# Turning gathered expert tokens with VectorE and two DMAs instead of TensorE, in one fused attention and expert block

## The chip, the core and the metric

The kernel runs on one core of one Trainium2 chip. The metric is device microseconds (us) of one execution. A core has TensorE (PE in the profile; PEld are its weight loads), VectorE (DVE), ScalarE (ACT), GpSimd (POOL), SyncE (SP, which here only issues DMAs) and 16 DMA engines. Every engine runs its own instructions in the order in which the program gives them, and waits for others through semaphores.

## What is computed

One transformer block on x of shape (16, 256, 256) in float32: an attention part, then a part with eight experts, in which each expert takes the 512 tokens with its highest gate values out of 4096 tokens. Only the second part is touched:

```python
# x: (4096, 256) tokens after attention; E = 8 experts, DD = 1024
gate = softmax(tok @ Wgate.T, axis=-1)
vals, idx = top_k(gate.T, 512)                  # for each expert, its 512 tokens
g = ln(tok[idx], mlp_g, mlp_b)                  # gathered, normalised, gain and bias
y = gelu(g @ fc1[e].T + b1[e]) @ fc2[e].T + b2[e]
tok = tok.at[idx].add(y * vals)                 # scattered back, added
```

The attention part (16 sequences of 256 tokens, 16 heads of 64) is the same before and after the change.

## The kernel before

The kernel is one program whose instructions are put in order by hand (a list of places for the attention part, a loop for the experts); the framework adds semaphores and changes no order.

The attention part takes the sequences one after another and writes two things to DRAM for each token: the token itself, to `out`, and its normalised form without gain and bias, to `xn_dram` (4096 rows of 1 KB).

The expert part is a list of 16 jobs (`Job`). A job is one expert with 256 of its 512 tokens. Jobs 0 to 7 use a first routing, over the tokens of the first 15 sequences; jobs 8 to 15 use a second routing over all tokens, which is worked out beside jobs 1 to 6. The steps of a job are these:

- `load`: SyncE issues three DMAs, 1 MB for the second weight matrix, 1 MB for the first, 128 KB for the bias. The weight tiles have two buffers, so the load for job k+2 waits until job k's matmuls are done.
- `gives` and `onehot` (VectorE): one 128x128 one-hot matrix for each 128 tokens (30 of them for a job of the first routing, 32 for one of the second), from which `list_matmul` (TensorE) and `take` (VectorE) make the list of the job's token numbers and gate values.
- `gather` (GpSimd): two indirect DMAs fetch 2 x 128 rows of `xn_dram`.
- `transposes` (TensorE): four 128x128 transposes turn the gathered tokens, and `evict` (ScalarE) applies gain and bias from PSUM to SBUF (tile `xT`).
- `up` and `gelu` (8 steps f), `down` (two halves i of four steps each), `weigh` and `finish` (VectorE): the two layers and the scaling.
- `scatter` (GpSimd): for each half i an indirect DMA that adds 128 rows to `out`.

The expert loop runs over the jobs. Each round k has 16 slots s, eight for `up` and eight for `down` of job k. Between them stand the steps for the next job (`new` = job k+1) and the one after (`far` = job k+2). `LIST_AT` = 5 is the slot in which the list of `new` is made and its gathers are issued, `TURN_AT` = 14 the slot in which its tokens are turned. The one-hots of `far` are laid out one step (two or three matrices) for each slot, from slot 6 of one round to slot 4 of the next; what is left is laid out in front of `list_matmul`. Round 7 is different (`late`): job 8 needs the second routing, and all its one-hots are made in slots 0 to 5 of that round, its list in slot `LATE_AT` = 7. The generator `rest` does the second routing in rounds 1 to 6. In every fifth slot it has VectorE choose two bits of the threshold from TensorE's last count and compare for the next two (lines 1060 to 1090), and TensorE counts five slots later (line 1075).

The attention part has the same kind of turn as the change uses: VectorE transposes 32x32 blocks (line 861), one store takes the tile to DRAM (`blocks`, line 869), and one load with rearranged rows brings it back (line 882).

Of the kernel before, what the change touches and what calls it, by code (L numbers as in the profile page):

```python
# [9 lines left out]
F32 = mybir.dt.float32  # L10
I32 = mybir.dt.int32
BF16 = mybir.dt.bfloat16
AF = mybir.ActivationFunctionType
# [5 lines left out]
P = 128  # L19
B, N, D = 16, 256, 256  # L20
H, HD = 16, 64
E, DD = 8, 1024
# [5 lines left out]
DC = D // P  # L28
HP = H // 2
FC = DD // P  # L30
KC = CAP // P
KL = KC // 2
CAPL = CAP // 2
NV = 5
SQ = 32
QB = P // SQ
# [2 lines left out]

LN1_G, LN1_B, B_ADA, MLP_G, MLP_B = 0, 2, 4, 6, 8  # L40
QN_G, QN_B, KN_G, KN_B, B1 = 10, 11, 12, 13, 14
NVEC = B1 + E * FC


class Plan:
# [7 lines left out]
    def step(self, place, engine, took, run, needs=(), makes=(), tiles=(), mode=0, lag=0.1):  # L53
        k = len(self.steps)
        self.steps.append((place, engine, took, run, needs, tiles, mode, lag))
        for m in makes:
            self.makers.setdefault(m, []).append(k)
# [7 lines left out]
def kernel(  # L65
# [6 lines left out]
    woutT: bass.AP,  # L72
    wgateT: bass.AP,
    fc1T: bass.AP,
    fc2T: bass.AP,
    b2s: bass.AP,
    vecs: bass.AP,
# [2 lines left out]
    nc = tc.nc  # L80

    const = ctx.enter_context(tc.tile_pool(name="const", bufs=1))
    dram = ctx.enter_context(tc.tile_pool(name="dram", bufs=1, space=DRAM))
# [6 lines left out]
    vec = const.tile([P, NVEC], F32, name="vec")  # L90
# [440 lines left out]
    if True:  # L531
        attw = ctx.enter_context(tc.tile_pool(name="attw", bufs=1))
        seq = ctx.enter_context(tc.tile_pool(name="seq", bufs=2))
        work = ctx.enter_context(tc.tile_pool(name="work", bufs=2))
# [146 lines left out]
        class Group:  # L681
# [91 lines left out]

            def back(self):
                if self.g < 2:
                    self.raw = work.tile([P, QB, TB, HP // 2, SQ], F32, tag="qraw", bufs=2, name="qraw")
                else:
                    self.raw = self.keys()[:, self.g - 2]
                raw = self.raw.rearrange("p k t h m -> p k (t h m)")
                nc.sync.dma_start(raw, self.blocks.rearrange("k d q n -> (d q) k n"))  # L780

            def affine(self):
                if self.g < 2:
                    qT = of_sequence(qTs, self.b, "qT", [P, HP, N])
                    for t in range(TB):
                        nc.scalar.activation(
                            qT[:, 4 * self.g : 4 * self.g + 4, bass.ts(t, P)].rearrange(
                                "p h (k m) -> p k h m", m=SQ
                            ),
                            self.raw[:, :, t], AF.Identity, bias=qgb[:, 1:2], scale=qgb[:, 0:1],  # L790
                        )
                    return
                kT = self.raw.rearrange("p k t h m -> p (k t h m)")
                nc.scalar.activation(
                    kT, kT, AF.Identity,
                    bias=vec[:, KN_B : KN_B + 1], scale=vec[:, KN_G : KN_G + 1],
                )
# [399 lines left out]
        class Job:  # L1197
            def __init__(self, e, routing, tiles):
                self.e, self.routing, self.tiles = e, routing, tiles
                self.oh = None  # L1200

            def load(self):


                e = self.e
                self.w2 = seq.tile([P, FC, D], F32, tag="oT", name="w2")
                nc.sync.dma_start(self.w2, fc2T[e].rearrange("(f p) d -> p f d", p=P))
                self.w1 = seq.tile([P, DC, DD], F32, tag="v", bufs=2, name="w1")
                nc.sync.dma_start(self.w1, fc1T[e].rearrange("(c p) f -> p c f", p=P))
                self.b2 = moe.tile([P, D], F32, tag="b2", bufs=2, name="b2")  # L1210
                nc.sync.dma_start(self.b2, b2s[:, bass.ts(e, D)].to_broadcast([P, D]))

# [65 lines left out]
            def evict(self):  # L1278
                self.xT = seq.tile([P, DC, CAPL], F32, tag="hT", name="xT")
                for c in range(DC):  # L1280
                    nc.scalar.activation(
                        self.xT[:, c, :], self.px[:, c, :], AF.Identity,
                        bias=vec[:, MLP_B + c : MLP_B + c + 1],
                        scale=vec[:, MLP_G + c : MLP_G + c + 1],
                    )
                self.hid = seq.tile([P, FC, CAPL], F32, tag="qT", name="hid")
                self.y = work.tile([P, KL, D], F32, tag="pr", bufs=PRB, name="y")
                self.ph, self.py = {}, {}

            def up(self, f):  # L1290
                self.ph[f] = ps.tile([P, CAPL], F32, tag="sc", bufs=4, name="ph")
                for c in range(DC):
                    nc.tensor.matmul(  # L1293
                        self.ph[f], self.w1[:, c, bass.ts(f, P)], self.xT[:, c, :],
                        start=(c == 0), stop=(c == DC - 1),
                    )

            def gelu(self, f):
                k = B1 + self.e * FC + f
                nc.scalar.activation(  # L1300
                    self.hid[:, f, :], self.ph[f], AF.Gelu_apprx_tanh,
                    bias=vec[:, k : k + 1], scale=1.0,
                )

            def down(self, i, a=0, b=FC):
# [51 lines left out]
        for b in range(B):  # L1357
# [6 lines left out]
            a = First(b)  # L1364
# [9 lines left out]
            for (g, t), p in GROUP.items():  # L1374
                p += base
                a = Group(b, g, t)
                n = (b, g, t)
# [27 lines left out]
            for d in range(HP // 2):  # L1405
                a = Quad(b, d)
                p = base + d * QUAD
                g = d // 2
                n = (b, d)
                po = ("po", 0) + n  # L1410
                for i in range(2):
                    q = p + 3 * i
                    m = n + (i,)
                    sums, pb, prT, blocks = ("sums",) + m, ("pb",) + m, ("prT",) + m, ("blocks",) + m
# [20 lines left out]
            for t in range(TB):  # L1435
                a = Tail(b, t)
                p = base + TAIL[t]
                n = (b, t)
# [52 lines left out]
        jobs = [Job(e, r, n) for r, n in ((first, n1), (second, NT)) for e in range(E)]  # L1491
        for n in range(2):
            at(ROUTE + 60 + n * 80, "SP", 1.5, jobs[n].load, (), [("w", n)], [("oT", B + n), ("v", B + n)], lag=6.0)
        for n in range(2):
            a = jobs[n]
            k = top + 10 + 20 * n
# [29 lines left out]
        for k in plan.order(PLACES):  # L1526
            plan.steps[k][3]()

        LIST_AT, TURN_AT, LATE_AT = 5, 14, 7
        SLOTS = 2 * FC  # L1530

        def second_routing():
# [15 lines left out]

        rest = second_routing()
        last = len(jobs) // 2 - 2  # L1550
        jobs[2].load()
        parts = iter(())
        for k in range(1, len(jobs)):
            a = jobs[k]
            new = jobs[k + 1] if k + 1 < len(jobs) else None
            far = jobs[k + 2] if k + 2 < len(jobs) else None
            late = k == last + 1
            for s in range(SLOTS):
                for step in next(rest, ()):
                    step()  # L1560
                if late and s == 0:
                    new.gives()
                if late and s < 6:
                    new.onehot(6 * s, 6 * s + 6)
                if new and s == (LATE_AT if late else LIST_AT):
                    for _ in () if late else parts:
                        pass
                    new.list_matmul(0, NT)
                    new.take()
                    new.gather()  # L1570
                    if k == 1:
                        jobs[0].scatter(by_end[1])
                if new and s == TURN_AT:
                    new.transposes()
                    new.evict()
                if not late and s < LIST_AT:
                    next(parts, None)
                if far and k != last and s > LIST_AT:
                    if s == LIST_AT + 1:
                        parts = lay_out(far)  # L1580
                    next(parts)
                if s < FC:
                    a.up(s)
                    a.gelu(s)
                    if s == FC - 1:
                        a.weigh()
                else:
                    i, q = divmod(s - FC, 4)
                    a.down(i, 2 * q, 2 * q + 2)
                    if q == 3:  # L1590
                        a.finish(i)
                        a.scatter(i)
            if far:
                far.load()
        assert next(rest, None) is None
# [50 lines left out]
```

## Time and profile before

| what | value |
|---|---|
| time, median of 3 runs | 1074.48 us (1072.66 to 1075.8) |
| profiled execution: time, span | 1075.44 us, 1073.7 us |
| TensorE matmul busy, share of the span | 1039.4 us, 97% |
| VectorE busy | 822.4 us, 77% |
| ScalarE busy | 588.9 us, 55% |
| GpSimd busy | 617.5 us, 58% |
| DMA, all queues | 246.85 MB, mean 230 GB/s |

The span is the time from the first instruction to the last; the execution's own time is 1.7 us longer. The expert rounds 1 to 15 lie between 835 and 1067 us of the span. Queue q1 carries the DMAs that SyncE issues, q0 the indirect ones of GpSimd. In the timeline a row is a run of equal instructions with its start and duration in us, and in brackets the idle time of the engine before it and what ended that.

### The profile page before, as it was taken

The page shows a single profiled execution, that of the slowest core. Times are in us where ns is not written, and L with a number is a line of the kernel's source. Part 1 is how long each engine was busy: PE and PEld are TensorE (multiplying, and loading weights), DVE is VectorE, ACT ScalarE, POOL GpSimd, SP SyncE. Part 2 cuts the span into 40 slices and gives each one's busy share as a digit, 9 for nine tenths or more (in the row PEclk, how much of TensorE's full clock was granted, in tenths as well). Part 3 has the DMA queues.
Part 4 walks back from the last instruction along what each step waited for, and adds up shares of the span by engine and source line. Part 5 has one row for each costly group of instructions (what it writes and reads, how often), then busy time and mean ns, then how long its engine had stood idle before and what let it go on. Part 6 is the DMA issues. An engine that isn't in the chain of part 4 may idle for free. (4 is left out here: it accounts for less than half of the span.)

```text
span 1073.7 us, 17767 instructions
## 1 busy us (share of the span) xinstructions
PE 1039.4 (97%) x5547; PEld 681.8 (64%) x5547; DVE 822.4 (77%) x2281; ACT 588.9 (55%) x1646; POOL 617.5 (58%) x997
## 2 busy tenths in 40 slices
PE   7899999999999999999999999999789999999996
PEld 4455656555554655656565565666468888888885
DVE  6667888989888898798888888888667588655440
ACT  1577676666666666575766667675503422333331
POOL 3666776778667686766767676674401433333332
PEclk7999999999999999999999999999999999999998
DMA  6014889888987898888888898889430656665661
GB/s 217 1 60 157 279 289 319 293 294 277 309 281 262 282 317 303 294 291 271 280 296 304 280 306 282 290 315 312 147 103 21 196 146 180 196 184 155 185 204 20
DMA packets 165005, 246.85 MB, mean 230 GB/s; under 512 B 9520, under 2 KB 135728, under 8 KB 164912
## 3 DMA queue, kind: packets, MB, share of 16 engines
q1 hardware_dynamic: 156992, 235.44, 64.7%
q0 software_dynamic: 6144, 8.39, 4.3%
q10 hardware_dynamic: 1776, 1.90, 0.5%
q8 instruction: 44, 0.72, 0.3%
q14 instruction: 49, 0.40, 0.1%
HBM read 140.84 MB, written 104.86 MB: 229 GB/s over the span
## 5 line engine op out<-in xcount | busy, mean ns | idle before, releaser
L693 PE MATMUL pm<-wq,hT 128*128 128x512 f32 x768 | 362.0, 609 | 7.0 <-DVE qk L730 4.2
L851 POOL TENSOR_SCALAR pr<-pr,sums 128x256 f32<-128x256 f32 x512 | 238.2, 485 | 97.2 <-DVE sums L847 90.8
L840 ACT ACTIVATE pr<-sc,nmax 128x256 f32<-128x256 f32 x512 | 237.8, 480 | 101.5 <-DVE nmax L827 77.6
L693 PEld LDWEIGHTS pm<-wq,hT 128*128 128x128 f32 x768 | 138.2, 191 | 162.5 <-issue 137.2
L103 POOL TENSOR_TENSOR ss<-ss,neghalf 128x8 f32<-128x8 f32 x128 | 210.7, 1646 | 10.7
L827 DVE TENSOR_REDUCE nmax<-sc 128x2 f32<-128x512 f32 x256 | 165.8, 676 | 14.3 <-PE sc L819 13.6
L861 DVE STREAM_TRANSPOSE pb<-pr 128x512 f32<-128x512 f32 x232 | 154.2, 687 | 7.4 <-POOL pr L851 6.9
L819 PE MATMUL sc<-kT,qT 64*128 64x256 f32 x1024 | 135.2, 394 | 0.0
L907 PE MATMUL po<-prT,v 128*64 128x256 f32 x1024 | 128.7, 389 | 2.9 <-DMA prT<-blocks 2.9
L706 ACT ACTIVATE sq<-pm 128x512 f32<-128x512 f32 x128 | 76.7, 604 | 92.0 <-PE pm L693 91.0
L819 PEld LDWEIGHTS sc<-kT,qT 64*128 64x128 f32 x1024 | 91.3, 186 | 46.9 <-issue 28.5
L1326 POOL DMA_INDIRECT out<-y,idx x32 | 51.1, 1597 | 120.1 <-DVE y L1320 66.2
L1293 PE MATMUL ph<-xT,w 128*128 128x256 f32 x512 | 117.6, 383 | 0.0
L1309 PE MATMUL py<-w,hid 128*128 128x256 f32 x512 | 116.3, 380 | 0.0
L933 PE MATMUL pw<-wo,oT 128*128 128x256 f32 x512 | 115.2, 381 | 0.0
L907 PEld LDWEIGHTS po<-prT,v 128*64 128x64 f32 x1024 | 66.8, 137 | 68.7 <-issue 19.3
L933 PEld LDWEIGHTS pw<-wo,oT 128*128 128x128 f32 x512 | 96.3, 190 | 21.0 <-issue 5.8
L840 ACT ACTIVATION_READ_ACCUMULATOR pr<-sc,nmax 128x1 f32 x512 | 108.0, 211 | 0.0
L730 DVE TENSOR_TENSOR qk<-pm,ss 128x512 f32<-128x512 f32 x128 | 89.7, 702 | 22.8 <-POOL ss L103 20.8
L1300 ACT ACTIVATE hid<-ph,vec 128x256 f32<-128x256 f32 x128 | 60.4, 474 | 84.2 <-PE ph L1293 77.2
L1309 PEld LDWEIGHTS py<-w,hid 128*128 128x128 f32 x512 | 95.6, 190 | 12.8
L1293 PEld LDWEIGHTS ph<-xT,w 128*128 128x128 f32 x512 | 95.5, 190 | 12.9
(142 smaller groups left out, 1081.6 us busy)
## 6 DMA issues: line engine op xcount, KB each, us to landing
blocks<-pb SPq DMA_DIRECT2D x116, 512.0 KB
prT<-blocks SPq DMA_DIRECT2D x116, 512.0 KB
kblocks<-kb SPq DMA_DIRECT2D x60, 512.0 KB
w<-in_fc2T SPq DMA_DIRECT2D x16, 1024.0 KB
w<-in_fc1T SPq DMA_DIRECT2D x16, 1024.0 KB
qraw<-kblocks SPq DMA_DIRECT2D x30, 512.0 KB
kT<-kblocks SPq DMA_DIRECT2D x30, 512.0 KB
out<-tok SPq DMA_DIRECT2D x32, 128.0 KB
```

Of the source, the lines that this page charges most:

```text
L103: nc.gpsimd.tensor_tensor(dst, src, neghalf[:, : src.shape[1]], ALU.pow)
L693: nc.tensor.matmul(self.pm, hTs[self.b][:, c, bass.ts(self.t, P)], wq[:, c, bass.ts(self.g, GW)], start=(c == 0), stop=(c == DC - 1),)
L730: engine.tensor_tensor(dst, src.rearrange("p (q e d) -> p q e d", q=QB, e=8), by_head(self.ss[:, 1, :]), ALU.mult,)
L819: nc.tensor.matmul(self.sc[i, j][:, t, :], qTs[self.b][rows, hp, bass.ts(t, P)], keys[rows, hp] if whole else keys[rows, hp // 4, hp % 4], ...
L827: nc.vector.tensor_reduce(self.nmax[i, j], self.sc[i, j], AX.X, ALU.max, negate=True)
L840: nc.scalar.activation(dst, src, AF.Exp, bias=self.nmax[i, j][:, t : t + 1], scale=1.0, accum_out=self.sums[i][:, 0, j, t : t + 1],)
L851: nc.gpsimd.tensor_scalar(self.pr[i, j][:, t, :], self.pr[i, j][:, t, :], self.sums[i][:, 1, j, t : t + 1], 1.0, ALU.mult, ALU.mult,)
L861: nc.vector.transpose(self.pb[i][:, :, :, j].rearrange("p k c t n -> p t k c n"), self.pr[i, j].rearrange("p t (k c m) -> p t k c m", c=TB ...
L907: nc.tensor.matmul(self.po[j * HD : (j + 1) * HD, i, :], vs[self.b][:, c, bass.ts(4 * self.d + 2 * i + j, HD)], prT[:, j, c] if (self.b, s ...
L933: nc.tensor.matmul(self.pw, oTs[self.b][:, hp // 2, self.t, hp % 2, :], wo[:, hp, :], start=(hp == 0), stop=(hp == HP - 1),)
L1293: nc.tensor.matmul(self.ph[f], self.w1[:, c, bass.ts(f, P)], self.xT[:, c, :], start=(c == 0), stop=(c == DC - 1),)
L1309: nc.tensor.matmul(self.py[i], self.hid[:, f, bass.ts(i, P)], self.w2[:, f, :], start=(f == 0), stop=(f == FC - 1),)
```

## The change

For twelve of the 16 jobs (3 to 7 and 9 to 15, `job.exchanged`), the four TensorE transposes are replaced by an exchange. VectorE turns 32x32 blocks of the gathered tokens (`turn`, two instructions of 128x256), SyncE stores the tile to DRAM (`away`, 256 KB in rows of 2 KB), waits for it, and loads it back with the blocks at their places (`back`, 256 KB in runs of 512 B). ScalarE then applies gain and bias in place (`affine`). The order of the features that this gives is another one, and the first weight matrix, the gain and the bias are laid out to match on the host. The order of tokens within a job's columns is put right by `gelu`'s access pattern.

The order in the loop changes as well. The list is made and the gathers are issued in slot 0 (round 1 stays at 5, round 7 at 7), `turn`, `away` and `back` stand in slot 6, `affine` in slot 13. The second scatter of a job is held back and issued in slot 0 of the next round, behind the gathers. In round 1 two steps of one-hots are laid out for each slot.

```diff
+            def turn(self):
+                self.xb = work.tile([P, QB, DC, KL, SQ], F32, tag="prT", bufs=4, name="xb")
+                for i in range(KL):
+                    nc.vector.transpose(
+                        self.xb[:, :, :, i].rearrange("p q c n -> p c q n"),
+                        self.xg[:, i].rearrange("p (c q m) -> p c q m", c=DC, m=SQ),
+                    )
+
+            def away(self):
+                self.blocks = dram.tile([QB, SQ, QB, P], F32, tag="xblocks", bufs=2, name="xblocks")
+                nc.sync.dma_start(
+                    self.blocks.rearrange("k m q n -> (k m) (q n)"),
+                    self.xb.rearrange("p q c i n -> p (q c i n)"),
+                )
+
+            def back(self):
+                self.xT = seq.tile([P, QB, DC, KL, SQ], F32, tag="hT", name="xT")
+                nc.sync.dma_start(
+                    self.xT.rearrange("p k c i n -> p k (c i n)"),
+                    self.blocks.rearrange("k m q n -> (m q) k n"),
+                )
+
+            def affine(self):
+                for c in range(DC):
+                    xT = self.xT[:, :, c].rearrange("p k i n -> p k (i n)")
+                    nc.scalar.activation(
+                        xT, xT, AF.Identity,
+                        bias=vec[:, MLP_BQ + c : MLP_BQ + c + 1],
+                        scale=vec[:, MLP_GQ + c : MLP_GQ + c + 1],
+                    )
+                self.outputs()
...
-        LIST_AT, TURN_AT, LATE_AT = 5, 14, 7
+        LIST_AT, TURN_AT, LATE_AT = 0, 14, 7
+        EXCHANGE = {6: ("turn", "away", "back"), 13: ("affine",)}
...
+        for k, job in enumerate(jobs):
+            job.exchanged = k > 2 and k != last + 2
         jobs[2].load()
         parts = iter(())
+        held = []
         for k in range(1, len(jobs)):
...
             late = k == last + 1
+            list_at = LATE_AT if late else 5 if k == 1 else LIST_AT
             for s in range(SLOTS):
...
-                if new and s == (LATE_AT if late else LIST_AT):
+                if new and s == list_at:
                     for _ in () if late else parts:
                         pass
                     new.list_matmul(0, NT)
@@
+                if s == 0:
+                    for step in held:
+                        step()
+                    held = []
+                if new and new.exchanged:
+                    for what in EXCHANGE.get(s, ()):
+                        getattr(new, what)()
+                elif new and s == TURN_AT:
                     new.transposes()
                     new.evict()
-                if not late and s < LIST_AT:
+                if not late and s < list_at:
                     next(parts, None)
-                if far and k != last and s > LIST_AT:
-                    if s == LIST_AT + 1:
+                if far and k != last and s > list_at:
+                    if s == list_at + 1:
                         parts = lay_out(far)
-                    next(parts)
+                    for _ in range(2 if k == 1 else 1):
+                        next(parts, None)
@@
                         a.finish(i)
-                        a.scatter(i)
+                        if new and i == KL - 1:
+                            held = [partial(a.scatter, i)]
+                        else:
+                            a.scatter(i)
```

More of the change, by code (lines that the diff above doesn't have):

```diff
@@ L41 @@
 QN_G, QN_B, KN_G, KN_B, B1 = 10, 11, 12, 13, 14
-NVEC = B1 + E * FC
+MLP_GQ = B1 + E * FC
+MLP_BQ = MLP_GQ + 2
+NVEC = MLP_GQ + 4
 class Plan:
@@ L74 @@
     fc1T: bass.AP,
+    fc1Q: bass.AP,
     fc2T: bass.AP,
@@ L1200, in __init__ @@
                 self.oh = None
+                self.exchanged = False
             def load(self):
@@ L1208, in load @@
                 self.w1 = seq.tile([P, DC, DD], F32, tag="v", bufs=2, name="w1")
-                nc.sync.dma_start(self.w1, fc1T[e].rearrange("(c p) f -> p c f", p=P))
+                rows = fc1Q if self.exchanged else fc1T
+                nc.sync.dma_start(self.w1, rows[e].rearrange("(c p) f -> p c f", p=P))
                 self.b2 = moe.tile([P, D], F32, tag="b2", bufs=2, name="b2")
@@ L1285, in evict, with outputs @@
                     )
+                self.outputs()
[26 more added lines that the diff above has]
+                    )
+                self.outputs()
+            def outputs(self):
                 self.hid = seq.tile([P, FC, CAPL], F32, tag="qT", name="hid")
@@ L1293, in up @@
                     nc.tensor.matmul(
-                        self.ph[f], self.w1[:, c, bass.ts(f, P)], self.xT[:, c, :],
+                        self.ph[f], self.w1[:, c, bass.ts(f, P)],
+                        self.xT[:, :, c].rearrange("p k i n -> p k (i n)") if self.exchanged else self.xT[:, c, :],
                         start=(c == 0), stop=(c == DC - 1),
@@ L1299, in gelu @@
                 k = B1 + self.e * FC + f
+                dst, src = self.hid[:, f, :], self.ph[f]
+                if self.exchanged:
+                    dst = dst.rearrange("p (i k n) -> p k i n", i=KL, n=SQ)
+                    src = src.rearrange("p (k i n) -> p k i n", i=KL, n=SQ)
                 nc.scalar.activation(
-                    self.hid[:, f, :], self.ph[f], AF.Gelu_apprx_tanh,
-                    bias=vec[:, k : k + 1], scale=1.0,
+                    dst, src, AF.Gelu_apprx_tanh, bias=vec[:, k : k + 1], scale=1.0
                 )
@@ L1572 @@
                         jobs[0].scatter(by_end[1])
-                if new and s == TURN_AT:
+                if s == 0:
[6 more added lines that the diff above has]
+                elif new and s == TURN_AT:
                     new.transposes()
                     new.evict()
-                if not late and s < LIST_AT:
+                if not late and s < list_at:
                     next(parts, None)
-                if far and k != last and s > LIST_AT:
-                    if s == LIST_AT + 1:
+                if far and k != last and s > list_at:
+                    if s == list_at + 1:
                         parts = lay_out(far)
-                    next(parts)
+                    for _ in range(2 if k == 1 else 1):
+                        next(parts, None)
                 if s < FC:
@@ L1607, in columns, with quarters @@
         return v.reshape(-1, P).T
+    def quarters(v):
+        v = v.reshape((DC, QB, P // QB) + v.shape[1:])
+        return v.swapaxes(1, 2).reshape((D,) + v.shape[3:])
     def twice(v):
@@ L1618 @@
             columns(a["b1s"]),
+            columns(quarters(a["mlp_g"])), columns(quarters(a["mlp_b"])),
         ],
@@ L1629 @@
         "fc1T": a["fc1s"].transpose(0, 2, 1),
+        "fc1Q": quarters(a["fc1s"].transpose(2, 0, 1)).swapaxes(0, 1),
         "fc2T": a["fc2s"].transpose(0, 2, 1),
```

## The prediction

> **What bounds the kernel now.** I read the page first (97% TensorE), then TensorE's waits in the expert part, its timeline over one round, the table of VectorE's busy time by round, and the DMA queues inside a round.
>
> TensorE's waits from 819 us to the end, all of them:
>
> ```profile
> PE pls L1249 <- DVE oh L1241: 0.4, 1, 0.4
> ```
>
> So in the expert part TensorE runs without a gap but for 0.4 us: what is taken from its queue shortens the span, and any new wait of TensorE lengthens it. One round (job 9, TensorE's timeline, 959.39 to 974.54):
>
> ```profile
> 959.39 4.48 PE L1293 MATMUL ph<-xT,w 128*128 128x256 f32 x20
> 963.71 0.95 PE L1249 MATMUL pls<-give,oh 128*128 128x10 bf16 x32
> 964.52 2.84 PE L1293 MATMUL ph<-xT,w 128*128 128x256 f32 x12
> 967.19 5.34 PE L1309 MATMUL py<-w,hid 128*128 128x256 f32 x24
> 972.37 0.60 PE L1274 MATMUL px<-ident,xg 128*128 128x128 f32 x4
> 972.81 1.89 PE L1309 MATMUL py<-w,hid 128*128 128x256 f32 x8
> 974.54 0.59 PE L1293 MATMUL ph<-xT,w 128*128 128x256 f32 x2
> ```
>
> A round is 15.15 us. The four transposes hold the queue from 972.37 to 972.81, 0.44 us, not the 0.60 of their overlapping records. The list takes 0.81.
>
> VectorE's busy time in rounds 2 to 5 (bounds are the weight loads' issues; second column busy us):
>
> ```profile
> 850.65:866.08 15.43, 12.96 (x77) 1.00 0.64 186
> 866.08:881.51 15.43, 12.95 (x77) 1.00 0.52 172
> 881.51:896.96 15.45, 13.34 (x83) 1.00 0.65 181
> 896.96:912.34 15.38, 13.77 (x83) 1.00 0.65 185
> ```
>
> Mean 13.25 of 15.42, with 2.2 idle; a quiet round such as 959.59 to 974.73 has 7.88 of 15.14. The difference is the second routing.
>
> The queues while round 8 (from 944.25) loads its weights, first 946.1 to 950.9, then 951 to 955:
>
> ```profile
> q1 hardware_dynamic: 1152, 1.69, 98.9%
> ...
> q0 software_dynamic: 240, 0.39, 39.3%
> q1 hardware_dynamic: 234, 0.43, 31.4%
> ```
>
> GpSimd issued a scatter at 946.08 (1.58 us), yet its queue q0 moves no packet before 951: the first answer has no q0 row at all. On idle DMA engines the scatter issued at 956.47 has its first packet about 2.1 us later and lands after 3.9. Under the load q0 thus starts 2.8 us late, and the DMA engines fall idle at 954.0, 9.8 us into the round.
>
> **The change part by part**, times from the round's start.
>
> *Removed*: 12 x 0.44 = 5.3 us of TensorE's queue, all on the path. ScalarE's two evictions become two `affine` of the same size (0.56 each) on an engine busy 4.8 of 15.1: nothing. A quiet round becomes 14.7, a busy one 15.0.
>
> *One-hots of job 9*: certain from the code. Round 7 lists in slot 7, so job 9's layout runs only in slots 8 to 15: eight of its 15 steps, 14 matrices. The other 18 are laid out in slot 0 of round 8, behind `finish(1)`, which itself waits for TensorE's last matmul of round 7. The timeline shows 32 matrices in 5.30 us, 0.166 each: 18 take 3.0 us, in which TensorE's next instruction, the list, waits. Before, five of these steps had slots 0 to 4. Cost 3.0 us, once. Elsewhere the 15 steps fit slots 1 to 15.
>
> *When the gathers land*: list result at 1.1 (0.2 to VectorE), `take` 0.15, gathers issued at 1.3 and 2.6 (1.0 us each, 0.3 between). They take 3.1 from issue to landing on idle DMA engines (those at 814 and 815) and 4.0 at the end of the load (the two from 950). Lower bound 2.6 + 3.1 = 5.7. But the second is issued later than the scatter at 1.8 that got no packet before 6.8, so its nearest row is that scatter: behind the weights, which the engines finish between 6.8 and 8.2. Then all were idle at 9.8, the scatter's share included. With the scatter behind the gathers (0.8 us: 128 rows over 16 engines at 0.10 us each) and 0.3 for the landing, I take 9.3; upper bound 10.2, if the order in q0 saves nothing.
>
> [...] The five loaded scatters that I looked at all waited, and I go by these rows.
>
> *VectorE, quiet rounds 9 to 14*: two transposes. The 128x512 one takes 0.69, so 128x256 takes between 0.35 and 0.69; I take 0.4, 0.8 for both. VectorE reaches `turn` early and stands there until 9.3. The first half can go before, the second ends at 9.8. Behind it stand 24 one-hots (4.0), `weigh` (0.5) and `finish(0)` (0.4): done at 14.7, just when TensorE wants to list. Beside the saving I charge 0.13 a round: 0.8.
>
> *VectorE, busy rounds 2 to 6*: work 13.25 + 0.8 = 14.05 and about 0.5 idle between `finish(1)` and `take` leave 0.4 of 15.0. VectorE gets to `turn` after `take` (1.3), `gives` 0.5, eight one-hots 1.3 and one or two rounds of bit choice at 2.0 (line 1081 at 881.92 to the last compare at 883.89): 5.1 to 7.1, up to 1 more where it waits for a count (longest 1.1). It stands there until 9.3, so 1.2 to 3.2. Behind it stand up to 8.5 us (22 one-hots 3.6, `weigh` and `finish` 0.9, two bit choices 4.0): the one-hots end at 18.3 at worst, 3.3 behind the list. A round that begins so late reaches `turn` late and waits little, since its weights were asked for before the stall. Laid out round by round this way, the waits at `turn` come to about 3.2, 0, 1.3, 1.3 and 0, 5.8 in all; less one slack of 0.4, 5.4 us of TensorE's waits. Bounds: 0.8 with gathers at 5.7 (0.8 us more work in rounds with little slack), about 8.0 with 10.2.
>
> *The exchange*: the trace's landing semaphores give 2.5 us for a 512 KB store on a quiet queue (723.14) and 1.6 for a 128 KB one (724.87), so 1.6 to 2.5 for 256 KB; I take 1.9. A 512 KB load in 512 runs of 1 KB took 3.3 (713.26); this one has as many runs of half the size: at most 3.3, at least the 1.6 of the small store, 3.0 taken. From 9.8: stored 11.7, back 14.8, first `affine` 15.5 with hops. TensorE wants `xT` after the next list, 14.7 + 0.8 = 15.5: just in time, by nothing. The last round has no list: 0.8 us of waiting, once. Behind the wait of `back` in SP's queue stands only the next load, free at 14.7 anyway. The 0.5 MB of traffic falls into DMA time that is idle from 9.8. The held scatter lies behind the gathers (3.9 instead of 1.8), and its landing, near 10.5, is still before the next scatter at about 11.7.
>
> *Sum*: -5.3 + 3.0 + 0.8 + 5.4 + 0.8 = +4.7, so 1080.1 on the profiled execution's 1075.44. The median of the runs is 0.96 lower: 1079.2 us.
>
> **The rivals.**
>
> *Gathers not held* (other side, not slower): they land by 7. VectorE hardly waits, the exchange ends near 13.3: -5.3 + 3.0 + 0.8 = -1.5, or -1.4 with the quiet rounds' rest: 1073.1. For it: the gathers are asked for while the weights' first packets run. Against: the scatter's missing row. It decides for landings below about 8.
>
> *The exchange is late*: store and load take 1 us more each, or gathers land at 10.2 and later. Then every quiet round waits for `xT` or its one-hots: the sum is +8 to +12, 1083 to 1087. For it: two stores in the full attention queue took 7.6 and 7.8 us. Against: after 9.8 the queues are empty.
>
> *The edits' waits stay off TensorE*: the busy rounds lose nothing because VectorE's 2.2 us of idle were real slack, and job 9's one-hots are hidden. Only the 5.3 is left: 1069.2. Against: VectorE's order puts those 18 one-hots behind TensorE's end.
>
> **How the numbers follow.** A measurement of this kernel can tell about 0.3%, 3.2 us: slower is above 1077.7, faster below 1071.3. The forecast (landing at 8.5 to 10) spans +2 to +8, chance 0.6, of which 0.14 is under 3.2. Gathers not held 0.22, all within 0.3%. Late exchange 0.13, slower. No waits 0.05, faster. So slower 0.46 + 0.13 = 0.59, the same 0.36, faster 0.05. The range reaches from the unheld case, 1073.0, into the late exchange, 1086.0; the forecast's own is 1076.5 to 1082.5.
>
> **What the next profile would show.** If right: L1274 left with a quarter of its records; TensorE waiting about 3 us once for `oh` at the list of round 8 and several times 1 to 3 us in rounds 3 to 6; DVE waiting for the DMA of `xg` in nearly every exchanged round; quiet rounds of 14.7 to 15.0. Wrong if q0 packets appear before 950 in such a round, if quiet rounds exceed 15.15, or if TensorE waits mainly in `up` for `xT`.

## The result, and the profile after

The changed kernel takes 1086.06 us (median of 4 runs, 1085.2 to 1088.55) beside 1073.57 us for the kernel before on the same chip: ratio 1.0119, interval 1.0092 to 1.0146, so 12.5 us slower. Forecast were 4.7 us slower, 1079.2, with a range up to 1086.0. The direction held; the added time was 7.8 us more than forecast.

Throughout, a round's length is the time from the end of its predecessor's last `py` matmul to the end of its own. Those of the two profiled executions, in us:

| round | 1 | 2 | 3 | 4 | 5 | 6 | 7 | 8 | 9 | 10 | 11 | 12 | 13 | 14 | 15 | sum |
|---|---|---|---|---|---|---|---|---|---|---|---|---|---|---|---|---|
| before | 15.44 | 15.42 | 15.43 | 15.45 | 15.38 | 16.97 | 15.14 | 15.14 | 15.14 | 15.14 | 15.14 | 15.14 | 15.14 | 15.14 | 13.81 | 229.0 |
| after | 15.43 | 15.84 | 18.59 | 15.49 | 16.25 | 20.18 | 15.14 | 19.29 | 14.70 | 14.70 | 14.71 | 15.05 | 15.44 | 15.83 | 13.81 | 240.5 |

The rounds account for 11.4 us: 7.7 in rounds 2 to 6, 4.15 in round 8, and -0.4 in rounds 9 to 15. (The two profiled executions differ by only 9.8, because round 1 happens to begin 1.6 us earlier in the one of after. Over the profiles of this study that start lies anywhere between 833 and 838 us, so kernels are compared by their rounds here. The 11.4 is one execution against one; the interval above is 9.9 to 15.7 us.)

TensorE's waits from 819 us to the end, kernel after (engine, line, waited for: total us, times, longest):

```profile
PE pls L1254 <- DVE oh L1246: 3.3, 4, 1.9
PE ph L1333 <- ACT xT L1318: 1.4, 2, 0.9
PE pc L1078 <- DVE reach L1071: 0.8, 2, 0.7
```

One row has become three, but together they come to 5.5 us. With 5.3 us of transposes saved, waits of 5.5 can't make rounds longer by 11.4. The first question is where the rest is.

A quiet round without disturbance (round 9), TensorE's timeline, kernel after:

```profile
969.67 0.95 PE L1254 MATMUL pls<-give,oh 128*128 128x10 bf16 x32
970.47 7.15 PE L1333 MATMUL ph<-xT,w 128*128 128x256 f32 x32
977.46 7.07 PE L1353 MATMUL py<-w,hid 128*128 128x256 f32 x32
```

No `px` row is left in it, and it takes 14.70: the saving of 0.44 is there. Round 8, the costliest, looks like this; below it stand TensorE's stretches over the same time (bounds | length, busy time, granted clock, DMA share, GB/s):

```profile
950.38 0.50 PE L1254 MATMUL pls<-give,oh 128*128 128x10 bf16 x14
951.29 2.95 PE L1254 MATMUL pls<-give,oh 128*128 128x10 bf16 x18 [0.41 <-DVE oh L1246]
954.15 8.77 PE L1333 MATMUL ph<-xT,w 128*128 128x256 f32 x32
```

```profile
952.00:954.00 2.00, 2.00 (x13) 1.00 0.84 231
954.00:956.00 2.00, 2.00 (x7) 0.51 1.08 382
956.00:958.00 2.00, 2.00 (x7) 0.64 1.01 405
958.00:960.00 2.00, 2.00 (x11) 1.00 0.81 209
```

Two things are hidden here. The list's 32 matmuls, 0.81 us of work, are spread from 950.38 to 954.15, because each of the last 18 comes when VectorE has made its one-hot; of these 2.96 us of waiting the view of waits shows only the 0.41 in front of a run, and the table of stretches calls the time busy. And the 32 `ph` matmuls behind it take 8.77 us instead of 7.15: the granted clock is at half from 954.04 for 3.41 us. That costs 1.6 to 1.7 us more. Such a half-clock stretch stands in rounds 3 (868.7), 6 (919.9) and 8 (954.0), each behind a stretched list (by 1.9, 2.6 and 3.0 us); the kernel before has none in its expert rounds.

VectorE in rounds 2 to 5, kernel after (bounds are the rounds'; second column busy us):

```profile
849.05:864.89 15.84, 11.27 (x65) 1.00 0.67 206
864.89:883.48 18.59, 15.26 (x92) 0.91 0.56 178
883.48:898.97 15.49, 12.42 (x75) 1.00 0.66 212
898.97:915.22 16.25, 14.33 (x85) 1.00 0.66 203
```

Mean 13.3 of 16.5: as much work as before (13.25), and 3.2 us idle instead of 2.2, while TensorE waits for its one-hots. Where it stands, in round 2:

```profile
857.24 0.45 DVE L1296 STREAM_TRANSPOSE xb<-xg 128x256 f32<-128x256 f32 x1 [2.19 <-DMA xg<-xn_dram,idx]
858.38 0.45 DVE L1296 STREAM_TRANSPOSE xb<-xg 128x256 f32<-128x256 f32 x1 [0.69 <-DMA xg<-xn_dram,idx]
```

Last, the queues under round 10's load of weights (the round begins at 984.53), first 986.4 to 990.2, then 990.3 to 994.3:

```profile
q1 hardware_dynamic: 1011, 1.21, 98.1%
...
q1 hardware_dynamic: 337, 0.89, 58.7%
q0 software_dynamic: 227, 0.38, 37.4%
```

The gathers were issued at 985.79 and 987.11. In the first window q0 moves nothing, as in the kernel before; the second gather lands at 993.45, 8.9 us into the round.

### The profile page after: what moved, and what is told of

It is laid out like the page before. It is cut to its first block, busy times and chain, and to the rows that moved or that the text cites. A ratio compares the mean times of both kernels' runs of the same rounds, so it can differ in the third digit from the quotient of the medians.

```text
span 1083.5 us, 17736 instructions
## 1 busy us (share of the span) xinstructions
PE 1044.3 (96%) x5499; PEld 681.7 (63%) x5499; DVE 828.9 (77%) x2305; ACT 588.8 (54%) x1646; POOL 615.2 (57%) x997
## 4 chain that ended last, share of the span: by engine, by line
PE 80%; DVE 8%; DMA 8%; issue 1%; POOL 1%; ACT 1%; POOLq 0%; SPq 0%; DVEq 0%; ACTq 0%
PE pm L696 30%; PE sc L822 11%; PE po L910 11%; PE pw L936 10%; PE ph L1333 7%; PE py L1353 5%; DMA xg<-xn_dram,idx 3%; DVE oh L1246 2%; DMA wq<-in_wqkvT 1%; PE pl L973 1%; DVE reach L1071 1%; PE pp L891 1%; PE pls L1254 1%; PE pg L962 1%; PE ph L659 1%
## 5 line engine op out<-in xcount | busy, mean ns | idle before, releaser
L854 POOL TENSOR_SCALAR pr<-pr,sums 128x256 f32<-128x256 f32 x512 | 237.0, 481 | 97.6 <-DVE sums L850 91.6
L830 DVE TENSOR_REDUCE nmax<-sc 128x2 f32<-128x512 f32 x256 | 165.7, 676 | 13.3 <-PE sc L822 12.4
L1333 PE MATMUL ph<-xT,w 128*128 128x256 f32 x512 | 121.0, 395 | 1.6 <-ACT xT L1318 1.4
L1333 PEld LDWEIGHTS ph<-xT,w 128*128 128x128 f32 x512 | 98.5, 197 | 16.8 <-ACT xT L1318 2.4
L1353 PEld LDWEIGHTS py<-w,hid 128*128 128x128 f32 x512 | 96.4, 190 | 13.7 <-issue 0.4
```

Of the source, the lines that this page charges most:

```text
L830: nc.vector.tensor_reduce(self.nmax[i, j], self.sc[i, j], AX.X, ALU.max, negate=True)
L854: nc.gpsimd.tensor_scalar(self.pr[i, j][:, t, :], self.pr[i, j][:, t, :], self.sums[i][:, 1, j, t : t + 1], 1.0, ALU.mult, ALU.mult,)
L1333: nc.tensor.matmul(self.ph[f], self.w1[:, c, bass.ts(f, P)], self.xT[:, :, c].rearrange("p k i n -> p k (i n)") if self.exchanged else sel ...
L1353: nc.tensor.matmul(self.py[i], self.hid[:, f, bass.ts(i, P)], self.w2[:, f, :], start=(f == 0), stop=(f == FC - 1),)
```

## The experiments

The standing theory behind the runs: what costs is VectorE's stand at `turn` until the gathers land and the late one-hots of job 9, each made worse by the clock that drops behind a stretched list. Rivals were that VectorE has no room for the work of `turn`, that the exchange is late, and that the new order in GpSimd's queue does harm. What the runs gave (rounds by the profile of one execution, us; "half" counts the 3.41 us stretches at half clock in rounds 2 to 15; a ratio is to executions of the kernel before on the same chip):

| run | rounds 2-6 | round 8 | rounds 9-15 | sum 1-15 | half | median, us | ratio to before, interval |
|---|---|---|---|---|---|---|---|
| before | 78.65 | 15.14 | 104.66 | 229.0 | 0 | 1073.6 to 1075.1 | |
| after | 86.36 | 19.29 | 104.25 | 240.5 | 3 | 1086.06 | 1.0119 [1.0092, 1.0146] |
| e1_layout | 86.29 | 14.70 | 109.97 | 241.5 | 4 | 1084.04 | 1.0083 [1.0063, 1.0102] |
| e2_fill | 86.47 | 17.76 | 103.68 | 238.5 | 2 | 1085.95, one run | |
| e3_order | 77.96 | 15.14 | 104.66 | 228.3 | 0 | 1074.11 | 0.9995 [0.9984, 1.0007] |
| e4_quiet | 78.64 | 14.70 | 103.44 | 227.4 | 0 | 1074.26 | 0.9997 [0.9987, 1.0006] |
| e5_weights | 83.61 | 14.70 | 107.18 | 237.7 | 2 | 1081.12 | 1.0054 [1.0037, 1.0071] |
| e6_turn10 | 87.72 | 14.70 | 103.77 | 238.1 | 2 | 1082.47, one run | |
| e7_fill36 | 86.08 | 14.70 | 105.49 | 236.9 | 1 | 1085.58, one run | |
| e8_quietw | 80.91 | 14.70 | 102.89 | 230.4 | 0 | 1076.71 | 1.0015 [0.9999, 1.003] |
| e9_best | 77.95 | 14.70 | 103.18 | 226.4 | 0 | 1073.31 | 0.9984 [0.9974, 0.9993] |
| e10_work | 78.65 | 15.14 | 104.66 | 229.0 | 0 | 1073.91, one run | |
| e11_wait | 86.65 | 15.14 | 104.66 | 237.0 | 2 | 1085.6, one run | |
| e12_best | 77.97 | 14.70 | 104.53 | 229.2 | 0 | 1074.79 | 0.9996 [0.9983, 1.0009] |

**e1_layout: job 9's one-hots in round 7's time.** In round 7 two steps are laid out for each slot.

```diff
-                    for _ in range(2 if k == 1 else 1):
+                    for _ in range(2 if k == 1 or late else 1):
```

> Changed kernel, but round 7 lays out two steps of job 9's one-hots for each slot, so that none is left for slot 0 of round 8. Clock theory (a wait of TensorE is paid twice: the wait, and then 3.4 us at half clock): round 8 goes from 19.3 to about 14.7 us, the half clock at 954 us is gone, the kernel is 4.6 us faster than the changed one. Rival, only the 18 one-hots cost (3.0 us as predicted) and the half clock has another cause: 2.9 us faster, the half clock stays.

Round 8 falls from 19.29 to 14.70, by 4.6: 2.96 of waiting and the clock's 1.6. The rest of the profiled execution is no copy of after's, since round 10 took 21.32. Its exchange's store landed 4.56 us after its issue instead of about 2.0, and TensorE waited for `xT`, then ran 6.8 us at half clock:

```profile
986.00 10.17 PE L1333 MATMUL ph<-xT,w 128*128 128x256 f32 x32 [3.47 <-ACT xT L1318]
```

That run was the slowest of the four (1088.27; the others 1082.5 to 1084.8). So the exchange has no room to spare: in this execution one late store cost 6.6 us.

**e2_fill: the wait of round 8 kept, the clock kept up.** In front of round 8's list stand 28 transposes of the identity, which nobody reads.

```diff
+                    if k == last + 2:
+                        fill(28)
                     new.list_matmul(0, NT)
```

> Changed kernel with 28 needless TensorE transposes (some 3.0 us at full clock) in front of round 8's list, so that TensorE works while VectorE makes the 18 one-hots. Clock theory: no half clock near 954 us, round 8 about 17.6 us instead of 19.3, so 1.7 less, although no wait is shortened. Rival (the clock falls for the DMA load or by chance, not because TensorE idles): half clock stays, round 8 at 19.3 or more.

TensorE's timeline of round 8:

```profile
953.14 3.22 PE L557 MATMUL fill<-ident 128*128 128x128 f32 x28
956.20 0.95 PE L1254 MATMUL pls<-give,oh 128*128 128x10 bf16 x32
957.00 7.15 PE L1333 MATMUL ph<-xT,w 128*128 128x256 f32 x32
```

The list begins as late as in after, but TensorE was at work until then, and `ph` takes 7.15 and not 8.77. The half clock of that round is gone, the other two are still there. So the 1.6 us belong to TensorE's having little to do at the stretched list, not to the load of weights or to what `ph` reads.

**e3_order: the new order alone**, no job exchanged (with e1's edit).

```diff
-            job.exchanged = k > 2 and k != last + 2
+            job.exchanged = False
```

> New order (list and gathers in slot 0, scatter held, job 9 laid out in time), but all tokens turned by TensorE as before: the exchange alone is undone. Theory (VectorE stands at the turn until the gathers land, and that is what rounds 2 to 6 lose): rounds 2 to 6 return to 78.7 us within 0.7 (86.4 in the changed kernel), quiet rounds 15.15, kernel within 1.5 us of the one before. Rival (the early list leaves VectorE too little room even without the turn): rounds 2 to 6 stay at 81 or more and half clocks remain, kernel 3 to 6 us slower than the one before.

TensorE has no wait at all in the expert rounds, and round 6 is 0.7 shorter than before. Gathers in slot 0, ahead of the held scatter, do no harm: 0.9995.

**e4_quiet: the exchange in quiet rounds alone.** Jobs 1 to 8 go as before, jobs 9 to 15 with the new order and the exchange (with e1's edit).

```diff
-            job.exchanged = k > 2 and k != last + 2
+            job.exchanged = k > last + 2
...
-            list_at = LATE_AT if late else 5 if k == 1 else LIST_AT
+            list_at = LATE_AT if late else 5 if k < last + 2 else LIST_AT
```

> Order and TensorE transposes as before in rounds 1 to 7, new order and exchange only for jobs 9 to 15, with job 9 laid out in time. Theory (the loss lies in rounds 2 to 6 and in job 9's layout): no half clock, rounds 8 to 11 at 14.7, rounds 12 to 14 at 14.7 to 15.8, kernel 0.5 to 3 us faster than the one before. Rival (the exchange itself is late in every round, as the second rival of the prediction had it): quiet rounds 15.2 to 16, kernel 1 to 5 us slower than the one before.

All of the loss is gone with the exchange of the busy rounds; seven times 0.44 is 3.1, and 1.65 of it remain in the profile (rounds 10, 14 and 15 give some back). By the runs no gain can be told: 0.9997, where 0.5 to 3 us were expected.

**e5_weights: weights behind the exchange.** The second matrix and bias of the next job, then the first matrix of the job after, are asked for in slot 8 instead of at the round's end (with e1's edit).

```diff
+                if s == 8:
+                    if new and k > 1:
+                        new.load2()
+                    if far:
+                        far.load1()
...
-            if far:
-                far.load()
```

> Changed kernel with job 9 laid out in time, and the weight loads moved behind the exchange in SyncE's queue (in slot 8 of a round: the second matrix and bias of the next job, then the first matrix of the job after that), so that no weights are ahead of the gathers. Theory (the gathers land late because the weights are ahead of them, VectorE stands for them, and the exchange has no room): gathers land about 6 us after a round's start instead of 9 to 10, quiet rounds all at 14.7, rounds 2 to 6 at 78 to 81 us in all instead of 86.4, at most one half clock in them, kernel 0 to 4 us faster than the one before. Rival (VectorE's own work and order set the pace of rounds 2 to 6, whenever the gathers land): rounds 2 to 6 stay at 84 or more.

Rounds 8 to 13 settle at 14.70, yet rounds 2 to 6 still lose 5.0 against before, with one list wait of 1.9 us and half clock behind it: 83.6, neither the 78 to 81 of the theory nor the 84 of its rival. The second gather of a busy round had its last packet 7.4 to 10.5 us into the round, instead of landing at about 6 as expected, now behind the tail of the weights asked for half a round earlier: the load was moved from one side of the gathers to the other. TensorE waited longest for `xT` (3.7 us in all, 2.4 of them in round 15, which took 18.20 with half clock behind the wait).

**e6_turn10: VectorE turns later.** In the busy rounds `turn` stands in slot 10 (with e1's edit), when the gathers have landed.

```diff
-                    for what in EXCHANGE.get(s, ()):
+                    for what in EXCHANGE.get(s if k > last else {6: -1, 10: 6}.get(s, s), ()):
```

> Changed kernel with job 9 laid out in time, and in rounds 2 to 6 the turn, the store and the load stand in slot 10 instead of 6; nothing else moves. VectorE then has four more slots of its other work in front of the turn. Theory (standing in order for the gathers costs rounds 2 to 6): rounds 2 to 6 fall from 86.4 to 80 to 83, the waits of the list in rounds 3 and 6 shrink below 0.5. Rival (VectorE has simply too much work there, or the exchange is what is late): 86 or more, and TensorE waits for xT in them.

```profile
PE ph L1333 <- ACT xT L1318: 8.2, 7, 2.4
PE pls L1254 <- DVE oh L1246: 0.9, 1, 0.9
```

The list's waits shrink from 3.3 to 0.9, and the waits for `xT` grow from 1.4 to 8.2: turned later, the tokens come back too late. Rounds 2 to 6 gain nothing (87.72), which is what its rival had (86 or more, with waits for `xT`). Of the two slots tried, 6 and 10, neither suits both engines; the slots between them were not run.

**e7_fill36: the clock kept up in rounds 3 and 6**, with 8 and 20 fill transposes ahead of their lists (and e1's edit).

```diff
+                    if k in (3, 6):
+                        fill(8 if k == 3 else 20)
                     new.list_matmul(0, NT)
```

> Changed kernel with job 9 laid out in time, and 8 and 20 needless TensorE transposes in front of the lists of rounds 3 and 6, where TensorE waits for one-hots. Clock theory: no half clock in rounds 2 to 8, round 3 at 16.9 instead of 18.6 and round 6 at 18.5 instead of 20.2, though no wait of the list goes away. Rival (the waits alone cost, the half clocks are from elsewhere): rounds 3 and 6 as before or longer by the transposes.

Round 3 falls from 18.59 to 16.91 and has no half clock any more: 1.7 again. Round 6 misses: the fill itself had to wait 1.74 us for VectorE (for `finish`, by the view of waits), the clock fell all the same, and the round took 21.64.

**e8_quietw: e4 with e5's weights.**

> Rounds 1 to 7 as before the change, exchange for jobs 9 to 15 only, and the weight loads behind the exchange (slot 8, as in the run on the weights). Theory: gathers land near 6, TensorE never waits for xT, rounds 8 to 14 all at 14.7, so 3.1 us less than before the change in the rounds, a ratio near 0.997; with the last round's wait gone too. Rival (the exchange has no room for other reasons than the weights): TensorE still waits in rounds 10 to 14, ratio 0.9995 as in the run on quiet rounds alone.

Five of rounds 8 to 13 take 14.70 and one 14.71, better than in e4, but rounds 2 to 7 lose 3.5 us: there the gathers, still in slot 5, now meet the weights of slot 8's order, and TensorE waited four times for `xg`, 2.4 us in all. No gain, 1.0015.

**e10_work and e11_wait: the work without the wait, and the wait without the work.** Both are e3_order with one addition in slot 6 of rounds 2 to 6 (the access patterns of the transpose are left out here).

```diff
 # e10_work
+                if 1 < k < last + 1 and s == 6:
+                    xb = work.tile([P, QB, DC, KL, SQ], F32, tag="prT", bufs=4, name="xb")
+                    for i in range(KL):
+                        nc.vector.transpose(xb[...], a.xg[...])
 # e11_wait
+                if 1 < k < last + 1 and s == 6:
+                    xb = work.tile([P, 2], F32, tag="prT", bufs=4, name="xb")
+                    nc.vector.tensor_copy(xb, new.xg[:, :, 0])
```

> New order alone, and in slot 6 of rounds 2 to 6 VectorE makes two more 128x256 transposes, of the current job's tokens, which have long landed: the work of turn without its wait (the output is used by nobody). Standing theory (the wait costs, not the work): rounds 2 to 6 sum to at most 79.5 (77.96 without the extra work), TensorE waits little for oh, no half clock. Rival (VectorE has no room for the work itself): 81 or more, with list waits of 1 us and more.

> New order alone, and in slot 6 of rounds 2 to 6 VectorE copies one column (128x2) of the next job's gathered tokens: the wait of turn without its work, without the exchange, and with TensorE turning the tokens as before (the copy is used by nobody). Standing theory (VectorE's stand until the gathers land is the cost): rounds 2 to 6 sum to 82 to 86, TensorE waits 1 to 3 us for oh in rounds 3, 4 or 6, and at least one half clock follows. Rival (the work or the late exchange is the cost): at most 79.

VectorE in rounds 2 to 5 of e10_work:

```profile
849.12:864.54 15.42, 13.60 (x79) 1.00 0.65 185
864.54:879.97 15.43, 13.48 (x79) 1.00 0.53 173
879.97:895.42 15.45, 13.88 (x86) 1.00 0.59 179
895.42:910.80 15.38, 13.84 (x82) 1.00 0.62 182
```

And of e11_wait, with what it waited for:

```profile
852.76:868.77 16.01, 11.01 (x68) 1.00 0.56 171
868.77:887.35 18.58, 14.82 (x91) 0.91 0.50 149
887.35:902.80 15.45, 11.32 (x70) 1.00 0.60 179
902.80:919.30 16.50, 14.03 (x86) 1.00 0.57 169
```

```profile
DVE xb L1628 <- DMA xg<-xn_dram,idx: 7.9, 3, 3.3
```

This pair decides. With the work added VectorE is busier (13.7 of 15.42) and rounds 2 to 6 lose 0.7 against e3_order, all of it in round 6. With one copied column, 0.2 us of work, VectorE is less busy (12.8 of 16.6), and the rounds lose 8.7, a little more than expected: TensorE transposes as before, nothing is exchanged, and rounds 2 to 6 are as long as in the whole change (86.65 beside 86.36). Rounds 3 and 6 take 18.59 and 20.10, in after 18.59 and 20.18. (That the execution of 1085.6 us is as long as the whole change's is chance: its round 1 began at 837.3 instead of 833.6, and its rounds sum to 237.0 instead of 240.5.)

**e9_best and e12_best: what the runs point to.** Jobs 3 to 8 are turned by TensorE, only jobs 9 to 15 exchanged, with the new order, e1's edit, and from round 8 on the weights behind the exchange. e12_best asks for job 9's second matrix too in slot 8 of round 8.

```diff
-            job.exchanged = k > 2 and k != last + 2
+            job.exchanged = k > last + 2
...
 # e12_best against e9_best
-                    if new and k > last + 2:
+                    if new and k > last + 1:
                         new.load2()
...
-            if far and k < last + 2:
+            if far and k <= last:
                 far.load()
+            elif k == last + 1:
+                far.load1()
```

> New order of the gathers everywhere; job 9 laid out in round 7's time (as in the run of the new order alone); TensorE turns the tokens up to job 8; only jobs 9 to 15 are exchanged; from round 8 on the weights are asked for behind the exchange, in slot 8. Standing theory (the added time lies in the busy rounds' wait at turn, in job 9's wait and in the clock drops behind both; the saving of 0.44 us in a quiet round is real): rounds 2 to 6 as in the new order alone, near 78.0; rounds 9 to 14 at 14.70 each; sum of rounds 1 to 15 near 225.3 against 229.0 before, so 1070 us, ratio 0.9965, faster by about what can be told. Rival (the quiet rounds give the saving back by an exchange that now and then is late, as in one round of the run with job 9 laid out in time): ratio 0.999 to 1.002, with waits of ph for xT.

e9_best is 1073.31 beside 1075.0, ratio 0.9984, interval 0.9974 to 0.9993: faster by 1.7 us, clear of 1 but half of what was expected by the ratio (0.9965; the rival said 0.999 to 1.002). By the profile it is 2.6; round 9 took 15.86 where 14.70 was expected, behind one wait of 0.55 us for `xT`, such as the rival named.

> The run with the new order everywhere and seven exchanged jobs, and now job 9's second matrix too is asked for behind the exchange, in slot 8 of round 8, instead of at that round's start. In that run TensorE waited once for xT (0.55 us at 959.0), and round 9 took 15.86 instead of 14.70; it is the only exchanged job whose gathers stood behind 2 MB of weights. Theory (the late landing of these gathers makes job 9's exchange late): round 9 at 14.70, no wait of ph for xT, sum of rounds 1 to 15 near 225.3, ratio near 0.9975. Rival (the first exchanged round is late for another cause, such as the chain of round 8's routing): round 9 again above 15.3, ratio 0.998 to 0.999.

Round 9 now takes 14.70, so the late landing of job 9's gathers was the cause there. But the edit did harm one round earlier. SyncE's and TensorE's timelines:

```profile
935.26 0.37 SPq L1222 DMA_DIRECT2D w<-in_fc1Q  x1
```

```profile
941.70 0.55 PE L1285 MATMUL px<-ident,xg 128*128 128x128 f32 x3 [0.90 <-DMA xg<-xn_dram,idx]
```

In e9_best the first matrix stands in SyncE's queue behind the second, whose buffer is free only at the round's end. Alone, it started when job 7's `up` was done, at 935.26, in the middle of job 8's gathers (issued at 934.73 and 936.05): they landed 5.6 us after issue instead of 2.8 to 3.5. Round 7 took 16.54 instead of 15.14. Rounds 13 to 15 also lost 2.5 us together, with the gathers of rounds 13 and 14 landing 7.0 to 7.8 us after issue (3.8 to 5.4 in e9_best); why the loads ran slower there is open. e12_best is no better than before.

## Why the prediction was wrong in size

- *Removed transposes, -5.3*: as forecast. L1274 (now L1279) has 16 records left of 64, and undisturbed quiet rounds take 14.70 against 15.14.
- *Gathers at 9.3 us into the round*: the number was right. Rounds 9 to 13 have the second one at 8.9 to 9.2 and once (round 12) at 10.2. Issue to landing is 6.3 to 8.3 us in those rounds and 2.8 in round 7, with no weights on the way. None of them came near the prediction's lower bound of 5.7, and the rival "gathers not held" is out. But the picture behind the number, a queue that waits until the weights are through, does not fit all rows. GpSimd issued a scatter at 864.08, 0.8 us ahead of round 3's load, and its 144 packets pass in the middle of that load (868.8 to 870.6; the weights' packets go on until 874):

```profile
q1 hardware_dynamic: 353, 0.39, 67.1%
q0 software_dynamic: 144, 0.13, 45.4%
```

Here q0 and q1 share the engines, with 45.4% and 67.1% in the same 1.8 us. What is late under a load is the start: counted through q0's packets (48 for a gather, 144 for a scatter), the first packet of the gathers in the quiet rounds 9 to 14 comes 4.4 to 4.9 us after issue, of this scatter 4.8 after, and on idle engines 1.7 to 2.2 after. Why the start is late, no run here tells.
- *Job 9's one-hots, 3.0 once*: the wait was 2.96. Missing is the clock behind it, 1.6 to 1.7. e1 took both away, e2 the second alone.
- *Busy rounds, 5.4*: the mechanism was right, and e11 shows that the stand alone is enough. Against e3_order its rounds lose 8.7, of which two half-clock stretches of 1.7 leave 5.3. In the changed kernel VectorE stood for `xg` 2.9, 0, 1.8, 1.2 and 0 us in rounds 2 to 6, 5.9 in all, where 3.2, 0, 1.3, 1.3 and 0 had been laid out. Its rounds 2 to 6 lose 7.7 net of five saved transposes (2.2), so 9.9; less the two clock stretches 6.5. The term was 1.1 short; the 0.7 that the work of `turn` costs alone in e10 would cover more than half of that, the rest is open.
- *Quiet rounds and the last, -2.6 + 0.8 + 0.8 = -1.0 for rounds 9 to 15*: measured -0.4. "Just in time, by nothing" was the right reading: rounds 9 to 11 lose nothing, rounds 12 to 14 lose 0.35, 0.74 and 1.13: round 12's gathers landed at 10.2, and a store of round 13 took 3.9 us (at 1038.5). So two of these rounds exceed the 15.15 that the prediction had named as a sign of being wrong. The last round waited for nothing. Store and load were forecast at 1.9 and 3.0; mostly they took 2.0 to 2.1 and 2.6 to 3.0. (The 3.3 us from which the load's bound came was misread: of that load's 16 landing signals the first came after 3.3 us and the last after 5.0.)

The sum: 4.7 forecast, plus 3 x 1.7 = 5.1 for the clock, 1.1 for the busy rounds and 0.6 for the others is 11.5, against 11.4 in the rounds. The step that failed is that the forecast took a wait of TensorE to cost its own length. It cost about 1.7 us more in each of the three rounds where it stretched the list by 1.9 us or more.

Of the tests named for the next profile, most held: the quarter of records, the 3 us at round 8's list, the list's waits in rounds 3 to 6, and VectorE waiting for `xg` (18 times, 45.9 us). The granted clock was not among them. The sign of q0 packets earlier than 5.6 us into a round (950 on the prediction's scale) did appear, in rounds 3 to 6 (from 4.0, 4.2, 5.3 and 4.75 us on) and in round 13 (2.5), each time for a scatter issued ahead of the gathers. The rival "exchange is late" (+8 to +12) names the right size with the wrong cause: waits for `xT` are 1.4 us in the changed kernel. It is what happens in e6.

Not settled: what makes a store late now and then. Of the 100 stores of the exchange in the profiles of this study, 11 took 3.2 us or more until `back` was issued behind them. During ten of these a 16 KB packet of the queue marked "instruction" passes, during the 89 shorter ones only five times. Two of the ten are in the changed kernel, at 960.34 (4.4 us, packet at 962.2) and 1038.46 (3.9, packet at 1039.3). No run here tells cause from chance.

## What to carry to other kernels

VectorE had slack here, and could still not afford to stand in the middle of its queue: it was not its share of busy time that counted but what was queued behind the wait (against e3_order, e10 with 13.7 of 15.42 us busy lost 0.7 us, e11 with 12.8 of 16.6 busy lost 8.7), and a copy of one column made rounds 2 to 6 as long as the whole exchange did (86.65 us beside 86.36), when it waited for the same transfer. To price a wait of TensorE, look whether it stretches a run of small matmuls such as the list, and whether the clock falls behind it; here that came to 1.6 to 1.7 us a time, on top of the wait. Before a consumer is moved ahead, ask when its data land under the load that is in flight at that place (here 6.3 to 8.3 us after issue, against 2.8 without weights on the way); where the load was moved here, the collision moved to another transfer (e5 still lost 5.0 us in rounds 2 to 6, e8 3.5 in rounds 2 to 7, e12 1.4 in round 7).

## What the runs showed of the hardware

- In the 14 profiles of this case (before, after and 12 runs) 13 lists are followed by a half-clock stretch. From the list's first matmul to the next `ph`, TensorE took 1.43 us (e11, round 3) to 3.8 us (e6, round 6) beyond the list's own 0.81 there, and the stretch (granted clock 0.50) begins 2.4 to 4.9 us after the list's start and lasts 3.41 us, or twice that (e1, round 10). Where it took 1.2 us beyond (after, round 5), 1.07 (e9, round 9) and 1.04 (after, round 14) there is none. Two further stretches follow waits in other places, of 2.4 us (e5, for `xT` in round 15) and 1.7 us (e7, in front of round 6's list). A wait of 1.9 us for `xT` in round 15 of e7 is followed by none.
- Ahead of the stretch of round 8 in the changed kernel TensorE stood still for 0.41 us in one piece, and issued 18 small matmuls in the 2.95 us behind that.
- A busy share of 1.00 said little here of small matmuls that wait one by one. The table of stretches shows 2.00 of 2.00 us busy from 952 to 954 with 13 matmuls, which back to back take 0.3 us.
- VectorE's 128x256 transpose took 0.40 to 0.45 us; 0.4 had been taken.
